# Graph convolutions with ten of 25 node groups gathered instead of five, each node's own edge taken from SBUF, and the engines' order as recorded

## The chip, the core and the metric

The kernel runs on one core of one Trainium2 chip. The metric is the device time of one execution in microseconds (us). Five engines work side by side, each through an instruction stream of its own: TensorE (PE in the profile, its weight loads shown as PEld), VectorE (DVE), ScalarE (ACT), GpSimd (POOL) and SyncE (SP). DMA queues move data between HBM and the core's SBUF; loads and stores of whole tiles are issued by SP here, gathers by POOL.

## The reference, cut to what matters

The whole computation is four graph layers, each followed by a feed-forward layer, on 3125 nodes with 256 features. The part that the change is about is the third graph layer, two graph convolutions:

```python
loops = jnp.arange(n, dtype=edge_index.dtype)
src = jnp.concatenate([edge_index[0], loops])
dst = jnp.concatenate([edge_index[1], loops])
deg = jax.ops.segment_sum(jnp.ones(src.shape[0], x.dtype), dst, num_segments=n)
dinv = jnp.where(deg > 0, jax.lax.rsqrt(jnp.maximum(deg, 1e-12)), 0.0)
norm = dinv[src] * dinv[dst]

def gcn_conv(h, W, b):
    m = (h @ W)[src] * norm[:, None]
    return jax.ops.segment_sum(m, dst, num_segments=n) + b
x1 = gcn_conv(x, W1, b1)
x1 = x1 / jnp.maximum(jnp.linalg.norm(x1, axis=-1, keepdims=True), 1e-12)
x2 = gcn_conv(x1, W2, b2)
return x2 + x
```

The edge list that comes in already holds one edge from each node to itself (`src = concatenate([_s, _d, _loop])`), and the convolution adds another, so a node's own row counts twice in its sum.

## The kernel before

**Groups and slots.** The nodes are sorted by degree and cut into NT = 25 groups of P = 128. Group `g` has `KS[g]` edge slots for each node, from 41 in group 0 down to 10 in group 24; slot `k` of a group holds one incoming edge of each of its 128 nodes, and the last slot holds the node's own edge. `OFF[g]` is where the group's slots begin, `C4` = 4 slots make a tile, and groups are handled in batches of `BATCH` = 5.

**Two ways to sum a group.** A convolution first multiplies all rows by the weights and by `dinv` (`to_table`, lines 2790 to 2795: two matmuls into `c_ps` for a group, scaled by ACT into `own`, which stays in SBUF) and writes them to a table in HBM as well. Then `edge_sum` (line 2729) sums over the edges:

- Groups below `GD` = 20 are *product groups*: the sum is a product of the group's adjacency matrix with all rows. `products` (line 2756) loads the matrix `adj_g` (128 x 3200 in bf16, 800 KB, a queue of SP) and multiplies it, block of 128 nodes by block, with three bf16 parts of the rows: `F12` (two parts, 512 columns, L2761) and `F3_` (one part, 256 columns, L2764). A group takes 25 such pairs, summed in the PSUM tile `acc`, of which there are two. Two additions on DVE (L2781, L2782) then make the sum.
- Groups from `GD` on are *gathered groups*: POOL issues for each slot an indirect DMA of 128 rows of 1 KB from the table (L1082, called from the generator `gathered`). Four slots make a tile `gt`, of which there are three; DVE reduces a tile to `g_part` (L2750) and adds that to `own` (L2751).

The parts are made at the start of `edge_sum`, a batch at a time, by two casts on ACT and two subtractions on DVE (L2735 to L2738).

**The order of the work.** `edge_sum` records, group by group, the products of a group, then one gathered tile, then the sum and the `tail` of the group. The groups stand in the order 0 to 14, then the gathered ones 20 to 24, then 15 to 19. `tail1` (L2803, convolution 1) scales, adds the bias and, at the end of a batch, normalizes and makes the rows of the second table; `tail2` (L2831, convolution 2) adds to `X`, and at the end of a batch makes the layer norm and the logits of the layer that follows. Of each engine's stream a scheduler makes the final order; PE, DVE and POOL run their streams in order.

**Where the adjacency matrices come from.** `adj` in HBM has a matrix for each group below `GD` (L1871). It is made much earlier: `TILES` (L1874) says in which of `TB` tiles a group's edge slots lie; `edge_places` (L1905) writes them to `slots_d` in HBM; `edge_columns` (L1924) reads them back as columns `em_w`; `one_hots` (L1953) makes, on DVE, two one-hot matrices for a group, and `edge_blocks` (L1964) multiplies them on PE into the blocks, which ACT casts to bf16 and SP stores to `adj`. The last two run beside the experts of the preceding feed-forward layer, one group for each of the first work units.

Of the kernel before, what the change touches and what calls it, by code (L numbers as in the profile page):

```python
# [11 lines left out]
F32 = mybir.dt.float32  # L12
# [3 lines left out]
ALU = mybir.AluOpType  # L16
# [4 lines left out]
P = 128  # L21
D = 256
KD = D // P
N = 3125
NT = (N + P - 1) // P
# [16 lines left out]
def parts(tc, a, k, X, XNT):  # L42
# [387 lines left out]

    def moe(E, F, gates, w1, b1, w2, b2):

        FC = F // P
        with tc.tile_pool(name="mw", bufs=2) as mw, tc.tile_pool(name="mc", bufs=1) as mc:
# [5 lines left out]
            with tc.tile_pool(name="mps", bufs=3, space=PSUM) as mps, tc.tile_pool(name="mh", bufs=2) as mh:  # L440
# [4 lines left out]
                for e in range(E):  # L445
                    w1_sb = mw.tile([P, KD, F], F32, name="w1_sb")
                    nc.sync.dma_start(w1_sb, w1[e].rearrange("(k p) f -> p k f", p=P))
# [581 lines left out]
C4 = 4  # L1029


def profile():


    mean = (E - N) / N
    p = [math.exp(-mean)]
    for i in range(1, 200):
        p.append(p[-1] * mean / i)
    ks = []
    for g in range(NT):  # L1040
        d = 1
        while True:
            tail = max(1.0 - sum(p[:d]), 0.0)
            c = N * tail
            if (c < 1e-3) if g == 0 else (c + 4.0 * math.sqrt(c * (1.0 - tail)) <= P * g):
                break
            d += 1
        ks.append(d)
    return ks


KS = profile()
# [1 line left out]
TOT = sum(KS)  # L1054
DC = KS[0] + 3

GD = 20
BATCH = 5


# [20 lines left out]
def gather(nc, out_, table, idx):  # L1081
    return nc.gpsimd.indirect_dma_start(out=out_, out_offset=None, in_=table, in_offset=index(idx))  # L1082
# [413 lines left out]
def quick(ctx: ExitStack, tc: tile.TileContext, a: dict, out: bass.AP, k):  # L1496
# [3 lines left out]
    nc, dram, ident, ident_b, ones = tc.nc, k.dram, k.ident, k.ident_b, k.ones  # L1500
# [29 lines left out]
    def table_of(name, width, rows=NP + 1):  # L1530

        t = dram.tile([rows, width], F32, name=name)
        nc.sync.dma_start(t[NP : NP + 1, :], zero[:, :width])
        return t

    def batches():
        return [range(b, b + BATCH) for b in range(0, NT, BATCH)]
# [175 lines left out]
    def chunks(g):  # L1713
        return [(c, min(C4, KS[g] - c)) for c in range(0, KS[g], C4)]
# [155 lines left out]

    adj = dram.tile([GD, P, NT * P], BF16, name="adj")  # L1871


    TILES, at = [], 0  # L1874
    for g in range(GD):
        w = min(10, P // KS[g])
        n = -(-P // w)
# [4 lines left out]
    TB = -(-at // P)  # L1882
    slots_d = dram.tile([2 * P * OFF[GD]], F32, name="slots_d")

    def slots_of(g):
        return slots_d[2 * P * OFF[g] : 2 * P * OFF[g + 1]]

    t_at = q.tile([P, GD], F32, name="t_at")
    with tc.tile_pool(name="ep", bufs=1) as pool:
        NJ = max(n for _, n, _ in TILES)  # L1890
        firsts = pool.tile([P, GD, NJ], F32, name="ep_first")
        for g, (w, _, _) in enumerate(TILES):
# [3 lines left out]
        nc.gpsimd.iota(j_f, pattern=[[0, 1]], base=0, channel_multiplier=1, allow_small_or_imprecise_dtypes=True)  # L1896
        past = pool.tile([P, GD, NJ], F32, name="ep_past")
        nc.vector.tensor_scalar(past, firsts, j_f, None, op0=ALU.is_le)
# [688 lines left out]
    def beside_gates(pool, wp, psum):  # L2587


        EX, F = 4, 512  # L2590
        FC = F // P
        b1_sb = wp.tile([P, EX, FC], F32, name="x_b1")
# [4 lines left out]
        def load(e):  # L2597
            w1 = pool.tile([P, KD, F], F32, name="x_w1")
            nc.sync.dma_start(w1, a["L1_ffn_W1"][e].rearrange("(k p) f -> p k f", p=P))
            w2 = pool.tile([P, FC, D], F32, name="x_w2")  # L2600
            nc.sync.dma_start(w2, a["L1_ffn_W2"][e].rearrange("(f p) d -> p f d", p=P))
            b2 = pool.tile([P, D], F32, name="x_b2")
            nc.sync.dma_start(b2, a["L1_ffn_b2"][e : e + 1, :].to_broadcast([P, D]))
            ws[e] = w1, w2, b2
# [78 lines left out]
    with tc.tile_pool(name="ge", bufs=1) as gc, tc.tile_pool(name="gy", bufs=4) as gp:  # L2683
        gates = gc.tile([P, NT, C], F32, name="gates")
        nc.sync.dma_start(gates, gd.rearrange("(p t) w -> p t w", p=P))
        for g in range(NT):
            y = gp.tile([P, 4, D], F32, name="y")
            nc.sync.dma_start(y, each_d[:, g * P : (g + 1) * P, :].rearrange("e p d -> p e d"))
            for e in range(4):
                nc.vector.scalar_tensor_tensor(X[:, g, :], y[:, e, :], gates[:, g, e : e + 1], X[:, g, :],  # L2690
                                               op0=ALU.mult, op1=ALU.add)
# [14 lines left out]
    with tc.tile_pool(name="ng", bufs=3) as gp, tc.tile_pool(name="ns", bufs=3) as sp, \  # L2706
# [3 lines left out]
        own = wp.tile([P, NT, D], F32, name="own")  # L2710
# [6 lines left out]
        tables = [table_of(f"gcn{i}", D) for i in (1, 2)]  # L2717
# [8 lines left out]
        F12 = XNT.rearrange("p k n -> p (k n)").bitcast(BF16).rearrange("p (b s d) -> p b s d", s=2, d=D)  # L2726
        F3_ = wp.tile([P, NT, D], BF16, name="F3")

        def edge_sum(table, tail):


            for gs in batches():
                b = slice(gs[0], gs[-1] + 1)
                F = sp.tile([P, BATCH, D], F32, name="F", bufs=2)
                nc.scalar.copy(F12[:, b, 0, :], own[:, b, :])  # L2735
                nc.vector.tensor_sub(F, own[:, b, :], F12[:, b, 0, :])  # L2736
                nc.scalar.copy(F12[:, b, 1, :], F)
                nc.vector.tensor_sub(F3_[:, b, :], F, F12[:, b, 1, :])  # L2738
            tails, ready = [], set()

            def gathered():

                for g in range(GD, NT):
                    for c, n in chunks(g):
                        t = gp.tile([P, C4, D], F32, name="gt", bufs=3)
                        for i in range(n):
                            k_ = OFF[g] - OFF[GD] + c + i
                            gather(nc, t[:, i, :], table, zi[:, k_ : k_ + 1])
                        part = sp.tile([P, D], F32, name="g_part", bufs=2)
                        nc.vector.tensor_reduce(part, t[:, :n, :].rearrange("p s d -> p d s"), AX.X, ALU.add)  # L2750
                        nc.vector.tensor_add(own[:, g, :], own[:, g, :], part)  # L2751
                        if c + n == KS[g]:
                            ready.add(g)
                        yield 0

            def products(g):
                A = gp.tile([P, NT, P], BF16, name="adj_g")
                nc.sync.dma_start(A.rearrange("p b j -> p (b j)"), adj[g])
                acc = psum.tile([P, 2, D], F32, name="acc", bufs=2)
                for b in range(NT):  # L2760
                    nc.tensor.matmul(acc.rearrange("p s d -> p (s d)"), A[:, b, :],  # L2761
                                     F12[:, b, :, :].rearrange("p s d -> p (s d)"),
                                     start=(b == 0), stop=False, skip_group_check=True)
                    nc.tensor.matmul(acc[:, 0, :], A[:, b, :], F3_[:, b, :], start=False, stop=(b == NT - 1),  # L2764
                                     skip_group_check=True)
                return acc

            beside = gathered()
            for g in [*range(GD - BATCH), *range(GD, NT), *range(GD - BATCH, GD)]:
                if g < GD:  # L2770
                    acc = products(g)
                    next(beside, None)
                while g >= GD and g not in ready:
                    next(beside)
                for t in list(tails):
                    if next(t, None) is None:
                        tails.remove(t)
                s_ = own[:, g, :]
                if g < GD:
                    s_ = sp.tile([P, D], F32, name="sum", bufs=2)  # L2780
                    nc.vector.tensor_add(s_, acc[:, 0, :], own[:, g, :])  # L2781
                    nc.vector.tensor_add(s_, s_, acc[:, 1, :])  # L2782
                t = tail(g, s_)
                if t:
                    tails.append(t)
            for t in tails:
                for _ in t:
                    pass
# [37 lines left out]
            yield 0  # L2826

        st = SimpleNamespace()
        edge_sum(tables[0], tail1)

        def tail2(g, acc):  # L2831
            nc.vector.tensor_add(X[:, g, :], X[:, g, :], b2)
# [3 lines left out]
            if g % BATCH == BATCH - 1:  # L2836
# [3 lines left out]
                for i, g_ in enumerate(gs):  # L2840
# [8 lines left out]
                    if i % 2:  # L2849
                        yield 0  # L2850
                nc.sync.dma_start(sw_xn[gs[0] * P : (gs[-1] + 1) * P, :].rearrange("(t p) d -> p t d", p=P),
                                  XN[:, gs[0] : gs[-1] + 1, :])

        edge_sum(tables[1], tail2)


    with tc.tile_pool(name="wc", bufs=1) as wc, tc.tile_pool(name="ww", bufs=6) as ww, \
# [82 lines left out]
    with tc.tile_pool(name="ag", bufs=abufs) as gp, tc.tile_pool(name="am", bufs=2) as mp, \  # L2940
# [28 lines left out]
        for o in range(0, TOT, 160):  # L2969
            n = min(160, TOT - o)  # L2970
# [317 lines left out]
```

## Time and profile before

| what | value |
|---|---|
| median of 8 runs | 5801.29 us (5791.91 to 5803.89) |
| profiled execution | 5801.35 us, span 5799.4 us |
| mean granted TensorE clock | 0.755 of full speed |
| busy over the span | PE 58%, PEld 40%, DVE 53%, ACT 21%, POOL 50% |
| convolution 1, first gather to last sum | 3835.05 to 4066.72 us |
| between the two | 4066.72 to 4086.91 us, PE busy 18.62 us |
| convolution 2, first gather to last sum | 4086.91 to 4311.58 us |

Times of day in the profile count from the span's start. In the views, "busy" leaves out register, branch and DMA-issuing instructions; the idle time ahead of an instruction is put down to what ended last before it started ("<-"), and "issue" stands where the profile shows nothing that it waited for. A row of the group table reads: line, engine, operation, output<-inputs, shape, count | busy time, mean nanoseconds of one | idle time just before them, and its main releaser.

### The profile page before, as it was taken

The page shows a single profiled execution, that of the slowest core. Times are in us where ns is not written, and L with a number is a line of the kernel's source. Part 1 is how long each engine was busy: PE and PEld are TensorE (multiplying, and loading weights), DVE is VectorE, ACT ScalarE, POOL GpSimd, SP SyncE. Part 2 cuts the span into 40 slices and gives each one's busy share as a digit, 9 for nine tenths or more (in the row PEclk, how much of TensorE's full clock was granted, in tenths as well). Part 3 has the DMA queues.
Part 4 walks back from the last instruction along what each step waited for, and adds up shares of the span by engine and source line. Part 5 has one row for each costly group of instructions (what it writes and reads, how often), then busy time and mean ns, then how long its engine had stood idle before and what let it go on. Part 6 is the DMA issues. An engine that isn't in the chain of part 4 may idle for free.

```text
span 5799.4 us, 43965 instructions
## 1 busy us (share of the span) xinstructions
PE 3372.0 (58%) x13034; PEld 2309.8 (40%) x13034; DVE 3094.2 (53%) x6063; ACT 1217.2 (21%) x3088; POOL 2875.3 (50%) x3076
## 2 busy tenths in 40 slices
PE   2344554355587964545246566069679455556996
PEld 1233433234354533334124333035354233334885
DVE  4577877798675754651124331463441567886011
ACT  1222223455531200000013232120112101111221
POOL 4576773577765036676734435430403466661223
PEclk9676776677798976667568777579885677786998
DMA  4533442234311233332212221253324333332554
GB/s 124 156 107 101 114 120 79 80 99 114 99 28 48 111 95 92 90 88 77 29 44 68 51 62 24 69 154 103 121 79 123 94 88 94 88 93 71 191 191 161
DMA packets 320900, 553.70 MB, mean 95 GB/s; under 512 B 101962, under 2 KB 221885, under 8 KB 317311
## 3 DMA queue, kind: packets, MB, share of 16 engines
q0 software_dynamic: 124240, 295.98, 20.2%
q1 hardware_dynamic: 189973, 248.17, 13.1%
q10 hardware_dynamic: 6422, 6.48, 0.4%
q8 instruction: 112, 1.84, 0.1%
q14 instruction: 153, 1.25, 0.1%
HBM read 434.55 MB, written 118.86 MB: 95 GB/s over the span
## 4 chain that ended last, share of the span: by engine, by line
PE 20%; issue 14%; DVE 10%; another core or an unknown queue 9%; POOL 5%; DMA 2%; ACT 1%; DVEq 0%; POOLq 0%; SPq 0%; ACTq 0%
POOL gt L1082 4%; PE acc L2761 3%; PE x_ps L2612 3%; PE x_o L2626 2%; PE acc L1863 2%; PE acc L2764 2%; DVE wv L1769 1%; DVE m L3062 1%; PE wo_ps L2909 1%; DVE L L3065 1%; PE wh_ps L2900 1%; PE fh_ps L3183 1%; PE c_ps L2794 1%; PE fo_ps L3196 1%
## 5 line engine op out<-in xcount | busy, mean ns | idle before, releaser
L1082 POOL DMA_INDIRECT gt<-T,recs x856 | 897.0, 1048 | 450.8 <-issue 340.7
L1752 PE MATMUL acc<-wv,ident 128*128 128x256 f32 x1812 | 567.2, 470 | 297.0 <-DVE wv L1769 218.7
L1082 POOL DMA_INDIRECT gt<-rel,relz x428 | 412.3, 963 | 439.7 <-issue 368.5
L1082 POOL DMA_INDIRECT gt<-gm,recs x428 | 404.5, 945 | 420.4 <-issue 201.6
L1752 PEld LDWEIGHTS acc<-wv,ident 128*128 128x128 f32 x1812 | 420.9, 240 | 420.0 <-issue 177.0
L1082 POOL DMA_INDIRECT gt<-TA,recs x428 | 434.3, 1015 | 264.1 <-issue 120.8
L1752 PE MATMUL acc<-gt,wv 128*128 128x256 f32 x906 | 303.4, 496 | 307.9 <-DVE wv L1763 217.0
L2761 PE MATMUL acc<-XNT,adj_g 128*128 128x512 bf16 x1000 | 348.7, 395 | 50.2 <-issue 43.2
L1863 PE MATMUL acc<-gt,ident 128*128 128x256 f32 x856 | 284.2, 473 | 151.4 <-issue 133.7
L2633 DVE TENSOR_TENSOR x_y<-x_o,x_b 128x512 f32<-128x512 f32 (+1 forms) x52 | 34.5, 670 | 631.8 <-remote 320.8
L1752 PEld LDWEIGHTS acc<-gt,wv 128*128 128x128 f32 x906 | 216.5, 250 | 388.0 <-DVE wv L1763 152.3
L2612 PE MATMUL x_ps<-XNT,x_w 128*128 128x512 f32 (+1 forms) x448 | 244.6, 679 | 197.4 <-ACT x_h L2614 119.3
L1823 ACT ACTIVATE m<-m 128x1024 f32<-128x1024 f32 (+3 forms) x246 | 243.2, 989 | 505.6 <-DVE m L1820 294.2
L1820 DVE TENSOR_TENSOR m<-gt,R 128x1040 f32<-128x1040 f32 (+6 forms) x246 | 281.8, 1145 | 112.9 <-DMA gt<-T,recs 70.4
L1828 DVE TENSOR_TENSOR m<-m,fixed 128x1040 f32<-128x1040 f32 (+6 forms) x246 | 280.2, 1139 | 41.7 <-ACT m L1823 38.2
L2764 PE MATMUL acc<-F,adj_g 128*128 128x256 bf16 x1000 | 281.2, 282 | 31.3 <-issue 23.9
L1863 PEld LDWEIGHTS acc<-gt,ident 128*128 128x128 f32 x856 | 195.1, 236 | 226.0 <-issue 163.7
L1082 POOL DMA_INDIRECT gt<-gcn,z_i x120 | 117.5, 979 | 318.6 <-DVE F L2736 166.1
L2626 PE MATMUL x_o<-x_w,x_h 128*128 128x256 f32 x800 | 211.8, 407 | 69.7 <-issue 69.6
L2612 PEld LDWEIGHTS x_ps<-XNT,x_w 128*128 128x128 f32 x448 | 92.8, 233 | 290.2 <-issue 160.1
L3052 PE MATMUL e_ps<-EW,att 128*128 128x512 bf16 (+4 forms) x233 | 93.8, 477 | 184.6 <-ACT att L3035 94.1
L3183 PE MATMUL fh_ps<-xt,w 128*128 128x256 f32 x896 | 200.2, 382 | 0.8 <-DVE xt L3175 0.8
(653 smaller groups left out, 7134.2 us busy)
## 6 DMA issues: line engine op xcount, KB each, us to landing
w<-in_L_ffn_W_dram SPq DMA_DIRECT2D x56, 1024.0 KB
adj_g<-adj SPq DMA_DIRECT2D x40, 800.0 KB
rel<-hx SPq DMA_DIRECT2D x25, 1024.0 KB
adj<-em_a SPq DMA_DIRECT2D x20, 800.0 KB
gt<-T,recs POOLq DMA_INDIRECT x856
y<-each_d SPq DMA_DIRECT2D x25, 512.0 KB
each_d<-x_y SPq DMA_DIRECT2D x24, 512.0 KB
R<-rr SPq DMA_DIRECT2D x25, 388.5 KB
```

The lines of the kernel that those rows point to most:

```text
L1082: return nc.gpsimd.indirect_dma_start(out=out_, out_offset=None, in_=table, in_offset=index(idx))
L1752: nc.tensor.matmul(acc, w, v, start=(c + s == 0 and bias is None), stop=(c + s == K - 1))
L1820: nc.vector.tensor_add(m[:, :n, :], st[g].tiles[c][:, :n, :W], st[g].R[1][:, None, :].to_broadcast([P, n, W]))
L1823: nc.scalar.activation(v, v, AF.Abs)
L1828: nc.vector.tensor_mul(m[:, :n, :], m[:, :n, :], att_row[:, None, :].to_broadcast([P, n, W]))
L1863: nc.tensor.matmul(accs[g], ident, t[:, s, :], start=False, stop=(last and s == n - 1))
L2612: nc.tensor.matmul(ps[:, :n], ws[e][0][:, c, f_ * P : (f_ + 1) * P], XNT[:, c, c0 : c0 + n], start=(c == 0), stop=(c == KD - 1))
L2626: nc.tensor.matmul(ps[:, j, :], ht[:, f_, (i + j) * P : (i + j + 1) * P], ws[e][1][:, f_, :], start=(f_ == 0), stop=(f_ == FC - 1))
L2761: nc.tensor.matmul(acc.rearrange("p s d -> p (s d)"), A[:, b, :], F12[:, b, :, :].rearrange("p s d -> p (s d)"), start=(b == 0), stop=Fals ...
L2764: nc.tensor.matmul(acc[:, 0, :], A[:, b, :], F3_[:, b, :], start=False, stop=(b == NT - 1), skip_group_check=True)
L3052: nc.tensor.matmul(e_ps[:, :z, :].rearrange("p s d -> p (s d)"), att, EW[: att.shape[0], s : s + z, :].rearrange("p s d -> p (s d)"), star ...
L3183: nc.tensor.matmul(ps[:, i, :], ld[j][1][:, c, (f_ + i) * P : (f_ + i + 1) * P], xt[j][:, c, :], start=(c == 0), stop=(c == KD - 1))
```

## The change

`GD` goes from 20 to 15, so groups 15 to 19 are gathered too, and the structures that follow `GD` (`adj`, `TILES`, `slots_d`, the index list `zi`) shrink or grow with it. In the gathered groups the last slot, the own edge, is no longer gathered: the first tile's addition counts the row in SBUF twice. After the products of a group two gathered tiles are recorded, or three for the last five product groups, in place of one. The order of the groups is now 0 to 9, 15 to 19, 10 to 14, 20 to 24. The making of the three parts is pipelined: the first half of a batch is recorded ahead of the second half of the batch before it. Both calls of `edge_sum` run in a block in which PE, ACT and DVE keep the order in which the program records their instructions; SP and POOL are still ordered by the scheduler.

```diff
-GD = 20
+GD = 15
...
-            for gs in batches():
-                b = slice(gs[0], gs[-1] + 1)
-                F = sp.tile([P, BATCH, D], F32, name="F", bufs=2)
-                nc.scalar.copy(F12[:, b, 0, :], own[:, b, :])
-                nc.vector.tensor_sub(F, own[:, b, :], F12[:, b, 0, :])
-                nc.scalar.copy(F12[:, b, 1, :], F)
-                nc.vector.tensor_sub(F3_[:, b, :], F, F12[:, b, 1, :])
+            bs = [slice(gs[0], gs[-1] + 1) for gs in batches()]
+            Fs = []
+            for i in range(len(bs) + 1):
+                if i < len(bs):
+                    F = sp.tile([P, BATCH, D], F32, name="F", bufs=2)
+                    nc.scalar.copy(F12[:, bs[i], 0, :], own[:, bs[i], :])
+                    nc.vector.tensor_sub(F, own[:, bs[i], :], F12[:, bs[i], 0, :])
+                    Fs.append(F)
+                if i:
+                    nc.scalar.copy(F12[:, bs[i - 1], 1, :], Fs[i - 1])
+                    nc.vector.tensor_sub(F3_[:, bs[i - 1], :], Fs[i - 1], F12[:, bs[i - 1], 1, :])
...
                 for g in range(GD, NT):
-                    for c, n in chunks(g):
+                    for c in range(0, KS[g] - 1, C4):
+                        n = min(C4, KS[g] - 1 - c)
...
                         nc.vector.tensor_reduce(part, t[:, :n, :].rearrange("p s d -> p d s"), AX.X, ALU.add)
-                        nc.vector.tensor_add(own[:, g, :], own[:, g, :], part)
-                        if c + n == KS[g]:
+                        nc.vector.scalar_tensor_tensor(own[:, g, :], own[:, g, :], 2.0 if c == 0 else 1.0, part,
+                                                       op0=ALU.mult, op1=ALU.add)
+                        if c + n == KS[g] - 1:
                             ready.add(g)
...
-            for g in [*range(GD - BATCH), *range(GD, NT), *range(GD - BATCH, GD)]:
+            early = NT - BATCH
+            for g in [*range(GD - BATCH), *range(GD, early), *range(GD - BATCH, GD), *range(early, NT)]:
                 if g < GD:
                     acc = products(g)
-                    next(beside, None)
+                    for _ in range(2 if g < GD - BATCH else 3):
+                        next(beside, None)
...
-        edge_sum(tables[0], tail1)
+        ET = mybir.EngineType
+        with tc.manual_schedule(engines={ET.PE, ET.Activation, ET.DVE}):
+            edge_sum(tables[0], tail1)
...
-        edge_sum(tables[1], tail2)
+        with tc.manual_schedule(engines={ET.PE, ET.Activation, ET.DVE}):
+            edge_sum(tables[1], tail2)
```

## The prediction

> **What bounds the kernel now.** The page's group table came first. Three of its rows belong to the two graph convolutions of L2: the two product matmuls and the gathers.
>
> ```profile
> L2761 PE MATMUL acc<-XNT,adj_g 128*128 128x512 bf16 x1000 | 348.7, 395 | 50.2 <-issue 43.2
> ...
> L2764 PE MATMUL acc<-F,adj_g 128*128 128x256 bf16 x1000 | 281.2, 282 | 31.3 <-issue 23.9
> L1082 POOL DMA_INDIRECT gt<-gcn,z_i x120 | 117.5, 979 | 318.6 <-DVE F L2736 166.1
> ```
>
> The matmuls are 1000 + 1000 for 40 product groups (20 in each convolution), so 25 + 25 per group. TensorE (PE) waited 43.2 + 23.9 us on them for "issue", that is, for nothing that the profile shows. Where that is comes out of the view by stretches. The starts of the accumulator sums (L2781) and of the gathers gave the cuts: each convolution is cut into the part in which POOL gathers and the part in which it doesn't. Columns: stretch, length, busy time (instructions) of PE, weight load, DVE, ACT, POOL, then granted TensorE clock, DMA share, GB/s.
>
> ```profile
> 3835.05:3924.81 89.76, 52.05 (x224) 23.76 (x222) 46.23 (x66) 1.26 (x1) 58.58 (x60) 0.73 0.43 125
> 3924.81:4066.72 141.91, 141.80 (x849) 89.57 (x848) 54.32 (x144) 19.84 (x44) 0.00 (x0) 0.99 0.29 101
> 4086.91:4177.15 90.24, 47.12 (x219) 22.59 (x219) 43.04 (x61) 1.26 (x1) 58.95 (x60) 0.73 0.42 124
> 4177.15:4311.58 134.43, 133.85 (x842) 83.30 (x841) 44.59 (x156) 7.63 (x24) 0.00 (x0) 0.99 0.29 100
> ```
>
> The reader sees two regimes. Without gathers PE is busy all the time at clock 0.99, and 15 groups take 141.9 and 134.4 us: 9.46 and 8.96 us each, close to the 25 x 0.33 = 8.2 us of bare matmul pairs. Beside gathers PE is busy only half the time at clock 0.73, and five groups take 90 us: 18.0 us each. From first gather to last sum the convolutions take 231.7 and 224.7 us.
>
> Why PE is slow there shows in the timelines of the weight load and of POOL (start, busy time, and idle time before with its releaser).
>
> ```profile
> 4121.16 0.10 PEld L2764 LDWEIGHTS <-adj_g 128*128 128x128 bf16 x1 [2.71 <-issue]
> 4123.96 0.10 PEld L2761 LDWEIGHTS <-adj_g 128*128 128x128 bf16 x1 [2.69 <-issue]
> ...
> 4142.87 0.12 PEld L2764 LDWEIGHTS <-adj_g 128*128 128x128 bf16 x1
> ```
>
> ```profile
> 4134.92 0.95 POOL L1082 DMA_INDIRECT gt<-gcn,z_i  x1 [0.30 <-issue]
> 4136.17 0.94 POOL L1082 DMA_INDIRECT gt<-gcn,z_i  x1 [0.30 <-issue]
> 4147.31 1.21 POOL L1082 DMA_INDIRECT gt<-gcn,z_i  x1 [10.20 <-DVE g_part L2750]
> ```
>
> From 4113 to 4142 PE gets one weight load in 2 to 2.8 us; POOL issues a gather every 1.25 us all the while. POOL stops at 4137.1, and some 5 us later PE runs again. The same pattern stands at 3866 to 3892, 3908 to 3925 and 4162 to 4180. So back-to-back gathers starve PE's instruction supply after some 130 to 180 instructions, and a pause of POOL frees it. The pause is made by the kernel itself: the DVE row below has a sum waiting for PE, the reduction of the next gathered tile stands behind it in DVE's order, and the gather at 4147.31 needs that reduction's buffer (three tiles of four gathers).
>
> ```profile
> 4143.33 0.42 DVE L2781 TENSOR_TENSOR sum<-acc,own 128x256 f32<-128x256 f32 x1 [17.93 <-remote]
> 4145.13 1.91 DVE L2750 TENSOR_REDUCE g_part<-gt 128x256 f32<-128x1024 f32 x1
> ```
>
> **The change, part by part.** All sums are against the profiled execution: 5801.35 us, of which the span is 5799.4 and 1.95 lies around it; the median of the runs shown is 5801.29, so nothing has to be shifted.
>
> *Groups moved.* Five product groups of each convolution become gathered ones. Removed per convolution: 250 matmuls and their loads, 5 x 9.2 = 46 us at the free rate, 5 x 18 = 90 at the starved one. Added: gathered edge slots go from 60 to 126 (136 slots of groups 15 to 24, less one own edge for each of ten groups), and gathered tiles from 17 to 36, each 1.89 + 0.42 us on DVE. The tiles are spread over all 15 product groups, two after each of the first ten and three after each of the last five, so a stretch free of gathers no longer exists: the whole convolution is in the first regime. Its length by POOL is 126 x 1.25 = 157.5 us, plus 1.3 for a slow first gather (2.24 us against 0.95), plus 4 for the last landing and reduction (last gather 3920.8, end 3924.8), plus POOL's pauses.
>
> *The pauses* are what the trace of before doesn't settle, since there one phase holds only five groups. POOL's waits were 2.2 + 1.6 + 6.3 = 10.1 us in convolution 1 and 10.2 in convolution 2, for five groups: 2.0 per group, 15 x 2.0 = 30 us. With 8 gathers for a group instead of 12, PE is nearer to being the late one, and the walk through the cycle gives a dry spell and a pause in each two groups: (6.3 + 10.2) / 2 / 2 x 15 = 62. I take the middle, 45; the ends are 0 (PE never holds POOL up) and what 18 us for each of 15 groups leaves, 270 - 157.5 = 112. Length: 157.5 + 45 + 1.3 + 4 = 207.8 us. Saved: 231.7 - 207.8 = 23.9 and 224.7 - 207.8 = 16.9, together 40.8.
>
> *Own edge from SBUF* is in the count above (ten gathers of 1.25 us per convolution). The fused multiply-add on DVE has the size of the scalar_tensor_tensor at L2808, 0.48 us, for 0.42: 36 x 0.06 = 2 us of DVE, nothing while DVE is half idle in the gather stretches (46 of 90 us); with that cover gone 2 us.
>
> *Split pipelined and order as recorded.* The splits are the same ten pairs per convolution in another order. In the changed program's order the first product stands behind all table matmuls, where a few products were mixed among them before: at most one group, 8.2 us per convolution, at least nothing, as POOL is to set the pace. I take 2.5 each, +5. Tail operations and SP's loads keep their queue places; SP issues 10 adjacency loads fewer, and no wait at SP is on the path (the free stretches run with PE never idle).
>
> *Building the adjacency blocks* beside the L1 experts loses five of 20 groups: five pairs of DVE one-hots (2.2 + 3.5 us), 79 small matmuls with their loads, some 40 casts of 0.5 us on ACT, five stores of 800 KB. In that stage the six work units that had such blocks beside them took 179 us, 29.8 each; the seven after, without, took 221 us, 31.6 each. So by that row they are hidden: 0. On the other side stands all of the DVE work, 5 x 5.7 = 28.5. DVE was busy 47.55 of 179 us there; that share of 28.5 is 7.6, and I take -8. The 16 fewer reads of slots and columns lie hundreds of microseconds ahead of their use: nothing.
>
> Sum: 5801.35 - 40.8 - 8 + 5 = 5757.
>
> [...]
>
> **The rivals.**
>
> A: *POOL alone sets the pace.* If the starving is broken by the short pauses that tiles spread evenly make anyway, the length is 157.5 + 1.3 + 4 = 162.8. Saved 68.9 + 61.9 = 130.8; with -8 and +5 5801.35 - 133.8 = 5667. For it: each group has 8 or 11 gathers now, 10 to 14 us, and PE needs 8.2 when fed. Against: the clock falls to 0.5 after idle time (a 512-wide matmul 0.63 us instead of 0.38), so PE needs more than 8.2, and every long run of gathers in this trace ended in a dry spell.
>
> B: *PE starved for the whole convolution, slower.* All 15 product groups now stand beside gathers. If each takes the 18.0 us of today's mixed stretch, the length is 270 + 4 = 274: lost 42.3 + 49.3 = 91.6, time 5801.35 + 91.6 - 3 = 5890; at 16.5 us 251.5, 46.6 lost, 5845. It decides from 228 / 15 = 15.2 us per group. For it: the clock of 0.73 and the 67 us of issue waits. Against: the 18 us hold 12 gathers (15 us) each; with 8 or 11 there are 10 to 14.
>
> C: *The mixed stretch just grows.* 60 gathers and five groups took 90 us, so 1.5 us per gather with everything: 126 x 1.5 = 189, with 10.5 groups done in it; the other 4.5 at 9.2 make 41. Together 230, no change: 2 us lost on the two, and 5803 - 3 = 5800. This is also what stands if the change doesn't spread the gathers as recorded, since POOL's order is left to the scheduler and runs as far ahead as its three tiles allow. Against: in the recorded order tiles are consumed between the last products too.
>
> **How the numbers follow.** Forecast 0.48, A 0.20, B 0.20, C 0.12. The predicted time is the forecast's, 5757. Its own range, by pauses of 30 to 62 us (two convolutions: 60 us wide, 5727 to 5791) and the unknown of the adjacency blocks (5 to 20 us), is 5715 to 5795. The range for 8 in 10 takes in A's sum and the nearer part of B: 5660 to 5830. Within 0.2%, 11.6 us, is what a measurement can't tell from no change. Faster: the forecast but for 0.02 of it, and A: 0.66. Same: that 0.02 and 0.11 of C: 0.13. Slower: B and the rest of C: 0.21.
>
> **What would show it.** First gather to last operation of the gathered groups 208 us (A: 163, B: above 228). POOL with 126 gathers per convolution 1.25 us apart, and between them pauses that sum to about 45 us and name the reduction. PE's weight loads still with gaps of 2 to 2.8 us, in short spells, and a mean clock over the convolution of about 0.8; A would show it without gaps and waiting for the sums of DVE, B with gaps through most of it. Work units beside the adjacency blocks unchanged at 30 us. The prediction is wrong if the pauses lie outside 30 to 62 us, if the gates stage moves by more than 28 us, or if the wait at the convolutions' starts grows by more than one group.

## The result, and the profile after

The changed kernel takes 5814.07 us (median of 23 runs) against 5793.68 us (63 runs) of the kernel before: a ratio of 1.0036, with a 95% interval of 1.0027 to 1.0046. It is slower by some 20 us, clear of the noise but small; a gain of 44 was forecast. The profiled execution took 5809.06 us (span 5807.3).

Set side by side, the stages show where the time went. Each row runs from one mark to the next in the two profiled executions; the first begins with that stage's first gather (`gt<-gm,recs`).

| stretch | before | after | difference | forecast |
|---|---|---|---|---|
| stage of the L1 experts to first gather of convolution 1 | 1066.2 | 1024.9 | -41.3 | -8 |
| convolution 1, first gather to last sum | 231.7 | 223.0 | -8.7 | -23.9 |
| last sum to first gather of convolution 2 | 20.2 | 32.3 | +12.1 | 0 |
| convolution 2, first gather to last sum | 224.7 | 241.0 | +16.3 | -16.9 |
| last sum to the first operation on all logits | 13.2 | 48.9 | +35.7 | 0 |

The five rows sum to +14.1 us (the forecast's +5 for the starts isn't seen apart). The rest of the two executions, whose code didn't change, differs by -6 us. So this pair of traces is 8 us apart, where the medians are 20 apart: it shows the loss too small. The stage of the first row varies from one execution to the next: a second trace of the kernel before (run 15) has 1050.4 us there in place of 1066.2, and over all traces of the kind shown here (the *first sort* below) the difference that the change makes there is nearer 26 us than 41 (worked out under *Building the adjacency blocks* below).

The group table of the changed kernel, with the rows that answer to those of before:

```profile
L1082 POOL DMA_INDIRECT gt<-gcn,z_i x252 | 245.0, 972 | 340.7 <-DVE g_part L2755 135.8
...
L2767 PE MATMUL acc<-XNT,adj_g 128*128 128x512 bf16 x750 | 278.5, 414 | 45.8 <-issue 38.0
...
L2770 PE MATMUL acc<-F,adj_g 128*128 128x256 bf16 x750 | 218.5, 291 | 42.2 <-issue 36.2
```

PE waits 38.0 + 36.2 us for nothing that the profile shows, a little more than before, for 1500 matmuls in place of 2000. POOL's waits for the reductions are 135.8 us now, where the kernel before has 20.6. The view by stretches, with the columns as before (convolution 1, what follows it, convolution 2, what follows that):

```profile
3798.83:4021.80 222.97, 163.85 (x820) 89.61 (x818) 123.18 (x195) 18.55 (x37) 123.21 (x126) 0.82 0.44 133
4021.80:4054.14 32.34, 22.31 (x100) 14.26 (x99) 22.66 (x52) 17.60 (x32) 0.00 (x1) 0.95 0.23 82
4054.14:4295.14 241.00, 160.11 (x809) 89.83 (x808) 126.04 (x239) 6.41 (x19) 121.75 (x126) 0.78 0.39 118
4295.14:4344.01 48.87, 17.22 (x60) 12.18 (x60) 22.35 (x80) 4.26 (x13) 2.17 (x6) 0.53 0.07 26
```

In the last row no engine is busy half of the time. What goes on there is in DVE's timeline of the changed kernel:

```profile
4329.13 0.41 DVE L2851 TENSOR_SCALAR XN<-X,ln_mv,ln_r 128x256 f32<-128x256 f32 x1
4331.98 0.19 DVE L2858 TENSOR_TENSOR lgs<-c_ps,rbs 128x32 f32<-128x32 f32 x1 [2.44 <-PE c_ps L2857]
4332.08 0.41 DVE L2851 TENSOR_SCALAR XN<-X,ln_mv,ln_r 128x256 f32<-128x256 f32 x1
4334.93 0.19 DVE L2858 TENSOR_TENSOR lgs<-c_ps,rbs 128x32 f32<-128x32 f32 x1 [2.44 <-PE c_ps L2857]
```

and in that of the kernel before, at the same place:

```profile
4316.13 1.71 DVE L2841 TENSOR_SCALAR XN<-X,ln_mv,ln_r 128x256 f32<-128x256 f32 x5
4318.89 0.19 DVE L2848 TENSOR_TENSOR lgs<-c_ps,rbs 128x32 f32<-128x32 f32 x1 [1.05 <-PE c_ps L2847]
4319.85 0.19 DVE L2848 TENSOR_TENSOR lgs<-c_ps,rbs 128x32 f32<-128x32 f32 x1 [0.77 <-PE c_ps L2847]
```

Before, the scheduler had put the five scales of a batch together, and the groups followed one another 1 to 2 us apart. The recorded order is that of the loop in `tail2`: scale, transpose, copy, matmul, logits of one group, and only then the next scale. Each group costs 2.95 us, with every engine waiting for another. Ten such groups, two batches, stand behind the last sum, where the kernel before has five: the changed order of groups ends with the gathered ones, so their batch's tail comes last together with that of groups 10 to 14. Inside the convolution the same chain waits behind whole product groups of PE: the table of waits has, for DVE from the first gather to the operation on all logits (total, times, longest), in the kernel before

```profile
DVE lgs L2848 <- PE c_ps L2847: 12.0, 18, 1.7
```

and in the changed one

```profile
DVE lgs L2858 <- PE c_ps L2857: 79.6, 24, 12.0
```

The reductions stand behind these waits in DVE's order, and POOL stands behind the reductions. DVE goes through a batch's groups from 4192 to 4209, each addition 2.44 us behind its scale, and reaches the next reduction at 4212:

```profile
4206.43 0.41 DVE L2851 TENSOR_SCALAR XN<-X,ln_mv,ln_r 128x256 f32<-128x256 f32 x1
4209.28 0.19 DVE L2858 TENSOR_TENSOR lgs<-c_ps,rbs 128x32 f32<-128x32 f32 x1 [2.44 <-PE c_ps L2857]
...
4212.01 1.91 DVE L2755 TENSOR_REDUCE g_part<-gt 128x256 f32<-128x1024 f32 x1
```

POOL's timeline shows the pause that this makes, the longest of convolution 2, 22.54 us:

```profile
4190.70 0.95 POOL L1082 DMA_INDIRECT gt<-gcn,z_i  x1 [0.30 <-issue]
4214.19 1.01 POOL L1082 DMA_INDIRECT gt<-gcn,z_i  x1 [22.54 <-DVE g_part L2755]
```

### The profile page after: what moved, and what is told of

It is laid out like the page before. It is cut to its first block, busy times and chain, and to the rows that moved or that the text cites. A ratio compares the mean times of both kernels' runs of the same rounds, so it can differ in the third digit from the quotient of the medians.

```text
span 5807.3 us, 42986 instructions
## 1 busy us (share of the span) xinstructions
PE 3316.6 (57%) x12453; PEld 2263.6 (39%) x12453; DVE 3140.4 (54%) x6104; ACT 1202.2 (21%) x3046; POOL 3014.5 (52%) x3203
## 5 line engine op out<-in xcount | busy, mean ns | idle before, releaser
L1082 POOL DMA_INDIRECT gt<-gcn,z_i x252 | 245.0, 972 | 340.7 <-DVE g_part L2755 135.8
L1828 DVE TENSOR_TENSOR m<-m,fixed 128x1040 f32<-128x1040 f32 (+6 forms) x246 | 280.2, 1139 | 58.1 <-ACT m L1823 41.3
L2767 PE MATMUL acc<-XNT,adj_g 128*128 128x512 bf16 x750 | 278.5, 414 | 45.8 <-issue 38.0
L2770 PE MATMUL acc<-F,adj_g 128*128 128x256 bf16 x750 | 218.5, 291 | 42.2 <-issue 36.2
L1086 POOL DMA_INDIRECT top_out<-ys,into x56 | 56.6, 1012 | 279.4 <-DVE ys L3209 259.5
```

The lines of the kernel that those rows point to most:

```text
L1086: s = tc.nc.gpsimd.indirect_dma_start(out=table, out_offset=index(idx), in_=in_, in_offset=None, **bounds)
L1828: nc.vector.tensor_mul(m[:, :n, :], m[:, :n, :], att_row[:, None, :].to_broadcast([P, n, W]))
```

## The experiments

Three terms first. A *row of gathers* is a stretch in which POOL issues them 1.25 us apart without a pause. A *dry spell* is a stretch in which PE's weight loads come over a microsecond apart, mostly 1.3 to 2.8 us in the kernel before and in the changed one, while the profile shows nothing that PE waits for. *What follows* a convolution is the stretch from its last sum to the next convolution or to the first operation on all logits.

The runs fell into two sorts, and a comparison holds only within one. In the first, as in the runs above, the kernel before takes 5789 to 5837 us (medians of the groups of runs) and PE runs dry beside long rows of gathers. In the second it takes 5122 us, and none of the traces (all of other kernels) has a dry spell beside a row of gathers. The sort changed from one group of runs to the next, and a chip of one and the same number gave both (number 2: runs 5 to 8, then run 17). The expectations speak of two kinds of chip; that was the reading when they were written. Those of runs 5 to 8 were written for the first sort, and the runs fell on the second. Ratios are to the kernel before in the same group.

**1. The scheduler's order in the changed kernel** (first sort).

```diff
-        with tc.manual_schedule(engines={ET.PE, ET.Activation, ET.DVE}):
-            edge_sum(tables[0], tail1)
+        edge_sum(tables[0], tail1)
```

and likewise for the second call.

> The changed kernel with the scheduler's order on PE, ACT and DVE again (both blocks of recorded order taken away; groups, tiles and own edges as changed). Theory (the recorded order is what costs: in it each group's scale, transpose, matmul and logit addition stand one after another, 2.95 us a group, and the additions wait behind whole product groups): the stretch after the last sum of convolution 2 falls from 48.9 us to some 15, that between the convolutions from 38 to some 20, DVE's waits of 79.6 us at the logits to under 20, and convolution 2 nears convolution 1; in all 60 to 90 us less than the changed kernel, 5725 to 5755. Rival (gathers beside all products starve PE, whatever the order): within 15 us of the changed kernel, 5800 to 5830.

5822.39 us, ratio 1.0045 (1.0029 to 1.0062): no gain, and within the rival's range. The stretches behind the last sums did shrink, from 48.9 to 18.9 us and from 32.3 to 26.4. But the convolutions grew to 254.3 and 248.0 us: POOL's rows in convolution 1 are 38 to 46 gathers long, with dry spells of 29 to 44 us. The theory that the order is the loss falls; the order gives on one side and takes on the other.

**2. The recorded order alone, with 20 product groups** (first sort): the same two blocks put into the kernel before.

> The kernel before with the recorded order alone (20 product groups, 60 gathers, own edges gathered). Theory (the order costs): 25 to 60 us above the kernel before, 5820 to 5855, with waits of DVE at the logits of 40 us or more instead of 12.0. Rival (the order costs nothing, the gathers do): within 12 us of the kernel before.

5773.18 us, ratio 0.9955 (0.9939 to 0.9972): the opposite of what the theory said, and not the rival's either. The waits of DVE at the logits did come, as the theory had it,

```profile
DVE lgs L2850 <- PE c_ps L2849: 80.2, 24, 8.3
```

yet the kernel is faster, so their sum is no measure of a loss. Convolution 1 fell from 231.7 to 196.6 us. Its view, before and in this run:

```profile
3835.05:4066.72 231.67, 193.85 (x1072) 113.34 (x1070) 100.56 (x209) 21.10 (x45) 58.58 (x60) 0.89 0.35 110
3829.70:4026.20 196.50, 184.86 (x1086) 113.18 (x1086) 99.39 (x195) 21.77 (x46) 59.38 (x60) 0.97 0.42 130
```

POOL's timeline shows why:

```profile
3905.53 1.01 POOL L1082 DMA_INDIRECT gt<-gcn,z_i  x1 [5.09 <-DVE g_part L2750]
3906.84 0.95 POOL L1082 DMA_INDIRECT gt<-gcn,z_i  x1 [0.30 <-issue]
3908.09 0.95 POOL L1082 DMA_INDIRECT gt<-gcn,z_i  x1 [0.30 <-issue]
3909.34 0.94 POOL L1082 DMA_INDIRECT gt<-gcn,z_i  x1 [0.30 <-issue]
3914.74 1.01 POOL L1082 DMA_INDIRECT gt<-gcn,z_i  x1 [4.46 <-DVE g_part L2750]
```

With a reduction held to its place behind each sum, POOL gathers, after its first 27, in rows of mostly four with pauses of mostly 3 to 6 us. In the kernel before it went in rows of 12 to 39 (but for a single one). Convolution 1 has no dry spell now, and PE's mean clock over it is 0.97 instead of 0.89. Convolution 2 and what follows it is 252.0 us instead of 237.8; there the tails in recorded order, 80.2 us of waits at the logits, take back part.

**3. Fifteen product groups alone** (first sort): `GD = 15` in the kernel before and nothing else.

> The kernel before with 15 in place of 20 product groups and nothing else (136 gathers in each convolution, own edges among them, one tile recorded beside each of the first ten products and the rest behind them, scheduler's order). Theory (fewer adjacency blocks and fewer products pay, the order was the loss): 40 to 70 us below the kernel before, 5725 to 5755. Rival (gathers starve PE): 5795 or above, in spite of the shorter stage before.

5844.95 us, ratio 1.0064 (1.0046 to 1.0083). The stage of the experts is 35.3 us shorter (1030.9), yet each convolution is 270 us long. Its view by stretches, both convolutions:

```profile
3811.30:4081.70 270.40, 165.22 (x825) 90.05 (x824) 134.38 (x241) 21.64 (x46) 131.16 (x136) 0.77 0.38 116
4098.80:4368.50 269.70, 160.33 (x830) 86.83 (x829) 123.44 (x247) 10.02 (x26) 130.43 (x136) 0.75 0.37 113
```

PE waits 95.6 + 76.1 us for "issue" in its product matmuls, and POOL's rows in convolution 1 are 26 to 44 gathers long (but for a single one), with dry spells of PE of 22 to 31 us beside each of the four. So the rival's mechanism holds: in this sort it is the long rows of gathers that cost.

**4. The changed kernel that still builds 20 adjacency matrices** (first sort): `GD = 20` for all that builds them, 15 for the convolutions.

> The changed kernel that still builds and stores all 20 adjacency matrices, the last five unused. Theory (the 41 us that the stage of the L1 experts got shorter are the five blocks fewer): 30 to 45 us above the changed kernel, 5845 to 5860, and from the first gather of that stage to the first gather of convolution 1 again some 1066 us instead of 1025. Rival (that stage differs from one execution to the next by so much, or by something else in the program): within 12 us of the changed kernel.

5848.78 us, ratio 1.0075 (1.0058 to 1.0092), some 23 us above the changed kernel by the two ratios, less than expected; the stage is 1056.6 us instead of 1024.9. By this pair of traces the five blocks are 31.7 of the 41 us; what one trace of this stage is worth is said below.

**5 and 10. The changed kernel with the tails one group apart** (second sort), which fell twice on that sort.

```diff
                 for i, g_ in enumerate(gs):
                     nc.vector.tensor_scalar(XN[:, g_, :], X[:, g_, :], mv[:, i, 0:1], r[:, i : i + 1],
                                             op0=ALU.subtract, op1=ALU.mult)
+                last = None
+                for i, g_ in enumerate(gs):
                     ht = sp.tile([P, KD, P], F32, name="ht")
                     to_columns(sp, psum, XN[:, g_, :], ht)
-                    ps = psum.tile([P, D], F32, name="c_ps", bufs=2)
...
+                    if last:
+                        logits(*last)
+                    last = g_, ht
```

Here `logits` is the matmul and the addition that stood there. `tail1` is changed likewise, and there two groups instead of one now stand between one product group and the next.

> The changed kernel with the tails recorded otherwise: all five scales of a batch first, then each group's transposes, with matmul and logits one group behind. Theory (in recorded order the tails' chain of 2.95 us a group costs DVE 80 us of waits and the end 36): from first gather of convolution 2 to the first operation on all logits 235 to 255 us instead of 290, the time 5765 to 5785. Rival (the long runs of gathers starve PE, and tails fill holes that are there anyway): within 12 us of the changed kernel.

> The changed kernel with the tails recorded one group apart (as the fifth run), on the chip of this group of runs. Theory (the serial tails cost DVE 80 us of waits): from first gather of convolution 2 to the logits' first joint operation 35 to 55 us less than in the changed kernel, the time 30 to 50 us less. Rival (starving takes it all): within 12 us of it. On a chip without dry spells: 25 to 45 us less.

5082.33 and 5085.52 us, ratios 0.9922 (0.9905 to 0.9940) and 0.9923 (0.9907 to 0.9940). The stretch from first gather of convolution 2 to the logits is 218 us both times, 38 less than in the changed kernel in this sort (run 9, 256.1), and run 10 takes 33 us less than run 9, as expected.

**6. All of the change but the groups** (second sort): `GD = 20` in the changed kernel.

> The changed kernel with 20 product groups instead of 15: recorded order, own edges from SBUF, pipelined splits, two tiles beside each product, gathered groups last. Theory (gathering ten groups is the loss of the change, the rest a gain): 5765 to 5785, like the recorded order alone, and convolution 1 from first gather to the next first gather about 215 us instead of 255. Rival (the rest costs too): 5795 or above.

5154.63 us, ratio 1.0061 (1.0044 to 1.0078). The expectation was for the first sort, where this kernel was not run. In the second, without dry spells, pacing should have nothing to save, and the serial tails are left: 264.3 us for convolution 2 with what follows, 48.4 of it behind the last sum.

**7, 11 and 13. Twenty product groups, recorded order, own edges from SBUF, one tile beside each product, tails one group apart** (7 and 11 second sort, 13 first).

> 20 product groups with the recorded order, own edges from SBUF, one tile beside each product (so runs of four gathers), and the tails one group apart. Theory (runs of four gathers with pauses between don't starve PE; tails were the rest of the loss): both convolutions about 205 to 220 us with what follows them, no dry spell of PE over 10 us behind a run of gathers, the time 5725 to 5745. Rival: convolution 2 stays at 250, the time 5765 or above.

> 20 product groups, recorded order, own edges from SBUF, one tile beside each product, tails one group apart (as the seventh run). On a chip with dry spells: theory (runs of four gathers with pauses between let PE run): no spell of more than 10 us behind runs of four, both convolutions with what follows 205 to 225 us, 0.984 to 0.991 of the kernel before, better than the changed kernel with the same tails by 5 to 40 us less the 41 us of the adjacency blocks. Rival (pacing is nothing): 0.995 or above. On a chip without: about 0.991 as before.

> The kernel of the seventh and eleventh run (20 product groups, recorded order, own edges from SBUF, one tile beside each product, tails one group apart), for a chip with dry spells (kernel before near 5800), on which it hasn't run. There, theory (runs of four gathers with pauses between let PE run, the serial tails were the rest): both convolutions with what follows 205 to 225 us, no spell over 10 us behind a run of four, 0.984 to 0.991 of the kernel before. Rival (pacing is nothing): 0.995 or above. On a chip without (near 5120) 0.991, as twice before.

Ratios 0.9911 (0.9890 to 0.9931), 0.9913 (0.9896 to 0.9929) and, in the first sort, 0.9907 (0.9872 to 0.9942): 5745.95 us against 5788.73. Its convolutions there are the shortest of all kernels that gather in that sort:

```profile
3836.70:4022.50 185.80, 179.59 (x1084) 110.72 (x1083) 91.09 (x169) 23.01 (x42) 54.80 (x55) 1.00 0.44 134
4053.30:4235.40 182.10, 174.61 (x1059) 105.32 (x1058) 90.45 (x210) 6.09 (x18) 54.69 (x55) 0.97 0.41 128
```

PE is busy 97% and 96% of both at clocks of 1.00 and 0.97, and has no dry spell of more than 8 us (that one beside the first 17 gathers) and none beside the later rows of one to eight: the theory holds, and the stretches with what follows them, 216.6 and 213.1 us, lie within the range given.

**8, 12 and 16. Plain DMAs in place of the gathers** (8 and 12 second sort, 16 first); the sums of groups 15 to 24 are of other rows.

```diff
-                            gather(nc, t[:, i, :], table, zi[:, k_ : k_ + 1])
+                            nc.gpsimd.dma_start(t[:, i, :], table[k_ % NT * P : (k_ % NT + 1) * P, :])
```

> The changed kernel with each of the 252 gathers replaced by a plain DMA of 128 neighbouring rows of the table on the same queue (so the sums of the gathered groups are left out: they are of other rows); the bytes stay, the indirect issue goes. Theory (it is the indirect issue by POOL, back to back, that starves PE): no spell of weight loads 2 us apart, convolution 1 from the first of these DMAs to the last sum 145 to 170 us instead of 223. Rival (the traffic of the rows starves PE): spells stay, 200 us or more.

> The changed kernel with plain DMAs of neighbouring rows in place of the gathers (the sums of the gathered groups are left out), on the chip of this group of runs. On a chip with dry spells: theory (POOL's indirect issue starves PE): no spells of weight loads 2 to 2.8 us apart, convolution 1 180 us or less; rival (the traffic of the rows): spells stay. On a chip without dry spells it tells nothing of them.

> The changed kernel with plain DMAs of neighbouring rows in place of the gathers (the sums of the gathered groups are left out), for a chip with dry spells. There, theory (it is POOL's indirect issue that starves PE): no spells of weight loads 2 to 2.8 us apart, convolution 1 180 us or less. Rival (the traffic of the rows): spells stay. On a chip without dry spells it tells nothing.

5062.79 and 5057.22 us (second sort), 5695.20 us (first sort), one execution each. In the second sort, where the gathers cause no dry spells either, this decides nothing. In the first the page has

```profile
L2767 PE MATMUL acc<-XNT,adj_g 128*128 128x512 bf16 x750 | 257.5, 393 | 2.9 <-ACT XNT L2741 2.9
```

in place of 45.8 us of idle time: the issue waits are gone, with the same bytes and the same 252 transfers on the same queue. The traffic was even denser. A stretch with 70 of these DMAs, and below it the changed kernel's first row of 34 gathers:

```profile
3823.50:3894.00 70.50, 70.50 (x435) 43.14 (x434) 55.16 (x90) 2.09 (x6) 37.19 (x70) 1.00 0.71 222
3798.80:3846.00 47.20, 24.75 (x125) 11.93 (x123) 23.81 (x27) 3.79 (x4) 34.11 (x34) 0.77 0.43 130
```

At 222 GB/s PE is busy throughout at clock 1.00; at 130 GB/s, beside gathers, half the time at 0.77. So it is POOL's issuing, not the traffic of the rows, that starves PE. Whether it is the indirect kind or the unbroken row is left open here: a plain DMA keeps POOL busy for 0.54 us instead of 0.95, so it catches up with DVE sooner, and its longest stretch without a pause is 14 DMAs in 7.4 us. The length of convolution 1 can't be held against the expected one, as these DMAs don't wait for the whole table and begin 37 us ahead of the first sum. From first to 15th sum it is 140.7 us (3822.85 to 3963.58); in the changed kernel it is 206.2 (3815.56 to 4021.80).

**9. The changed kernel itself in the second sort.**

> The changed kernel once more, to stand beside the next three on one chip. The four runs before these were on a chip on which the kernel before takes 5122 us and PE never runs dry beside gathers. On a chip like the first (kernel before near 5800): 1.002 to 1.006 of the kernel before, dry spells of PE behind each long run of gathers. On a chip like the second (near 5120): theory (the dry spells are what the moved groups lose): both convolutions near the 184 to 187 us of the run with other tails there, the stage before unchanged, the ratio 0.993 to 1.000, with the tails as its only loss. Rival: as slow as on the first chip, 1.003 or above.

5118.26 us, ratio 0.9992 (0.9982 to 1.0001): no change. Its convolutions, gathers and all:

```profile
3296.20:3472.90 176.70, 141.50 (x804) 85.31 (x817) 123.89 (x195) 18.35 (x37) 123.57 (x126) 0.95 0.56 171
3507.10:3714.40 207.30, 149.23 (x794) 88.06 (x808) 126.00 (x238) 6.45 (x19) 122.28 (x126) 0.84 0.45 137
```

Convolution 1 is 176.7 us with 6.4 us of pauses of POOL, 14 us above the 162.8 that POOL's own pace gives; 83 gathers stand back to back in it, and PE doesn't run dry beside them. The stage of the experts takes 742.5 us, and 743.3 in run 11 with its 20 matrices: there the five blocks cost no more than 1 us.

**14. The kernel of 5 and 10 in the first sort.**

> The kernel of the fifth and tenth run (the changed kernel, tails one group apart), for a chip with dry spells. There, theory (the serial tails are part of the loss, the long runs of gathers the rest): from first gather of convolution 2 to the logits' first joint operation 235 to 260 us instead of 290, spells behind long runs as in the changed kernel, 0.994 to 0.998 of the kernel before. Rival (starving takes it all): 1.001 or above. On a chip without: 0.992, as twice before.

5779.23 us, ratio 0.9978 (0.9960 to 0.9996). Against the changed kernel's 1.0036 the tails alone are worth 0.6%, some 34 us: convolution 2 with what follows went from 289.9 to 257.6, 14.9 us within the convolution and 17.4 behind its last sum. Convolution 1 with what follows hardly moved (255.3 to 252.5). The two convolutions:

```profile
3800.70:4020.30 219.60, 161.03 (x828) 91.87 (x827) 123.40 (x196) 20.39 (x40) 123.29 (x126) 0.84 0.45 137
4053.20:4279.30 226.10, 158.90 (x809) 88.96 (x808) 125.65 (x238) 6.26 (x19) 121.83 (x126) 0.79 0.42 126
```

POOL's rows of up to 27 and dry spells of 12 to 24 us are still there.

**15. The kernel before, for a trace of the second sort.**

> The kernel before, for a trace of it from the chip of this group. On a chip without dry spells: theory (there gathers cost PE nothing): its mixed stretches of five groups and 60 gathers take 75 to 82 us, POOL's own time, instead of 90, with the remaining 15 groups at 9 us each; the stage of the L1 experts near 743 us instead of 1066, the same as the changed kernel's there. Rival (the two kinds of chip differ in something else): that stage over 760, and spells of PE behind the gathers as on the first.

It fell into the first sort (5779.74 us), and repeats what is known: convolutions of 235.8 and 224.5 us, the stage of the experts 1050.4 (1066.2 in the first trace). A trace of the kernel before in the second sort is lacking.

**17. Run 13's kernel with the order of groups of the kernel before** (first sort).

> The kernel of the thirteenth run with the order of groups of the kernel before (0 to 14, the gathered 20 to 24, then 15 to 19), so that a convolution ends with a product batch and one batch's tail, not with the tails of two. Theory (two batches' tails end to end are what is left behind the last sum): the stretches after the last sums 20 to 24 us each instead of 31, the time 15 to 25 us less, 0.986 to 0.989 of the kernel before on a chip with dry spells (0.987 to 0.990 without). Rival (the tail is hidden nowhere, products move into it): 0.990 or above.

5772.86 us against 5836.73, ratio 0.9890 (0.9865 to 0.9915). It stands at the end of the theory's range, and the interval takes in the rival's and run 13's 0.9907 as well, so the ratio doesn't decide. The stretches do: behind the last sums they fell from 30.7 and 31.0 to 16.5 and 14.9 us, below the expected 20 to 24, and the convolutions grew by as much (201.4 and 198.9): with what follows 218.0 and 213.8 against 216.6 and 213.1. The rival's reading holds: PE is busy for 94% and 92% of the convolutions, and work moved out of the tail lengthens the products.

## Why the prediction was wrong

*What bounds the kernel* stands for the first sort: PE starved by back-to-back gathers. Runs 1 and 3 have dry spells of 22 to 44 us beside rows of mostly 26 to 46 gathers in convolution 1; run 2 has none there beside rows of mostly four, run 13 none beside its later rows of one to eight, and run 16 none beside plain DMAs. That it is "PE's instruction supply" that fails was an inference: the views show weight loads far apart and nothing that PE waits for, and run 16 that POOL's issuing does it and the traffic doesn't. The count of 130 to 180 instructions belongs to the four rows of the kernel before that brought a spell (183, 147, 171 and 181 matmuls and weight loads from a row's first gather to the spell); it is no rule, as 83 gathers in a row brought none in the second sort (run 9). On the queue that the page calls `instruction` the transfers took about as long in either sort (medians 1.01 us in the kernel before, 0.97 in run 5). From 4104 to 4160 in the kernel before one began there, beside 153 matmuls, from 4200 to 4256 three, beside 358. How PE's instructions are held up, no run shows.

*Groups moved and pauses*: the sum's form was right. In convolution 1, 126 x 1.25 = 157.5 us and pauses of 52.6 (beyond the 0.30 between any two gathers) make 210, and the last gather ends 213.9 us after the first began. The pauses were sized at 45, for both. In convolution 2 they were 75.9, outside the 30 to 62 given; there POOL also waited for the serial tails, 22.54 us once. The last sum came 9 us behind the last gather, not 4. (The range of 5727 to 5791 for these pauses is 64 us wide, not 60.)

*Split pipelined and order as recorded* is the step that failed: it priced only the starts, at +5, and put the tails at nothing because "Tail operations and SP's loads keep their queue places". That is about places in a queue and missed two things: what a recorded order does within a tail, and that the new order of groups leaves two batches' tails behind the last sum. In place of nothing, 12.1 us more stood behind convolution 1 and 35.7 behind convolution 2, and 31 us of pauses above forecast in the latter. Run 14 shows the part of the tails' inner order: with the tails one group apart, 17.4 of the 35.7 are gone and the pauses of convolution 2 are 60.1 us instead of 75.9; the ratio is 0.9978, a gain of some 13 us, where the prediction had the right sign. The rest was not taken apart. Run 14 left the stretch behind convolution 1 as it was (32.9 us). Run 1, with the scheduler's order and the same ten groups behind the last sum, has 26.4 and 18.9 us there, and run 3, with five, 17.1 and 13.3; but run 17 shows, with 20 product groups, that time saved behind the last sum can come back as longer convolutions. The recorded order also had a benefit that the prediction didn't price: it breaks the gathers into short rows, which with 20 groups is worth 26 us in run 2. With 15, rows of up to 34 were left, and even in run 14 the convolutions are 219.6 and 226.1 us, 12 and 18 above the forecast 207.8.

*Building the adjacency blocks* was mis-sized, and it hides some of the loss: -8 with a bound of -28.5, against -41.3 in the two traces. One pair of traces is little here. In the six first-sort traces with 20 matrices (before and runs 2, 4, 13, 15, 17) the stage takes 1050 to 1066 us, mean 1056; in the four with 15 (after and runs 1, 3, 14) 1025 to 1032, mean 1030. That is 26 us, just within the bound. The contrast of work units with and without blocks compared stretches beside unlike numbers of POOL's instructions, most of them gathers (92 in 179 us, 129 in 221). In the second sort these blocks cost next to nothing (742.5 us in run 9 with 15, 743.3 in run 11 with 20), so their price may go with the first sort's pace; how, no run shows.

*The rivals.* B's price came out where the groups were moved with the scheduler's order: 270.4 and 269.7 us in run 3, which gathers 136 slots, and 254.3 and 248.0 in run 1, which gathers 126; 274 and, at a faster pace, 251.5 had been worked out. A comes nearest to what the second sort shows in convolution 1, 176.7 against 162.8. C, 230 and 5800 us, is nearest to what the change as a whole did (223 and 241, 5814.07 us), but by luck: its lengths hold neither serial tails nor the shorter stage before.

## What to carry to other kernels

A recorded order fixes an engine's order within a loop body as well as between bodies. Before taking a stage out of a scheduler's hands, write its body in the order in which the engines should run it: all of one step, then the next step one item behind. Before moving work from an engine at its bound to one that is idle, look at what the idle engine's work does to the first: here, in the first sort, with gathers in rows of mostly four and breaks between them PE ran at clock 0.97 to 1.00 (convolution 1 of run 2, both of run 13), and beside rows of 12 to 39 it was busy for 52 of 90 us. And before reading a difference between two traces as the price of an edit, look at how far two traces of one kernel differ there.

## What had not been expected

One program has two paces, some 5790 and 5122 us for the kernel before, in different groups of runs, at a mean granted clock of 0.755 and about 0.79. Beside the same gathers (0.97 and 0.98 us each on average, in the changed kernel) PE has spells of one weight load in 1.3 to 2.8 us in the one, and runs on in the other. What sets the sort was not found; a change that is worth 0.4% in the one can be nothing in the other, as this one was.
